# A four-layer graph network on one core: five blocks of the third layer turned by VectorE in the second, and fetched

## The chip, the core and the metric

The kernel runs on one core of one Trainium2 chip. Its time is the device time of one launch in microseconds; "before" is 2893.02 us, the median of three runs between 2892.32 and 2893.67. A profile is taken of one more execution. Engines are named as the profile does: PE is TensorE, PEld its weight loads, DVE is VectorE, ACT is ScalarE, POOL is GpSimd, SP is SyncE, which here only issues DMAs.

## The reference, cut to what matters

Four attention layers over one graph of 4096 nodes with 256 features; each result is added to x and normalised. The third layer is the one that changes:

```python
def _L2_gnn_ref(x, adj, W, a):
    h = x @ W
    e_src = h @ a[:D, 0]
    e_dst = h @ a[D:, 0]
    e = e_src[:, None] + e_dst[None, :]
    e = jnp.where(e > 0, e, NEG_SLOPE * e)
    att_logits = jnp.where(adj > 0, e, MASK_VAL)
    attention = jax.nn.softmax(att_logits, axis=1)
    h_prime = attention @ h
    return jax.nn.elu(h_prime)
...
x = _layernorm(x + _L1_gnn_ref(x, adj, ...), axis=-1)     # second layer
x = _layernorm(x + _L2_gnn_ref(x, adj, ...), axis=-1)     # third layer
```

## The kernel before, in words

x lies in SBUF the whole time, as tile X: 128 partitions (P) by 32 tiles of 128 rows. Rows are also counted in 8 blocks (NB) of 512, four tiles (QB) each. Each layer runs over units (b, j): b is one of 8 blocks of outputs (a "pass"), j a tile of the nodes that are summed over; layers one, three and four have 32 units in a pass, layer two has 64. In each unit ScalarE computes exponentials or activations for 512 columns, VectorE multiplies them by the mask, and TensorE adds the products to sums in PSUM (the function sums).

The second layer (multi_head_attention) keeps LAG = 3 units between scores and sums. In its main loop the order on PE, DVE and ACT is the one in which the code issues the instructions. What is left of pass b-1 (row sums, division, normalisation) is strewn over units of pass b by finish: join_sums at units 7 and 9 (L706, one VectorE addition of 128x1024), row sums at 12, halves at 15 and 18, statistics, and four scale_row at 35, 37, 39 and 41, after which block b-1 of X has its final value of the layer. Block 7 is finished in the third layer, by tail. GpSimd adds the even products of a pass up (L683), and a DMA that accumulates (L689, den<-prob, issued by POOL) adds the odd ones; the two join_sums of the last pass are POOL's too.

The third layer (additive_one) needs x turned, features on partitions, for its projection. In pass 0, turn(n) has TensorE transpose a block: 8 transposes of 128x128 into two PSUM banks (L118), copied out by VectorE and ScalarE (L120). project(n) multiplies it by the weights (L196) and fills V, src and dst, from which unit (b, j) takes its j. fill_row(n) writes a block of src along the free dimension on all partitions: for n > 1 by a DMA to DRAM (L441) and another one that spreads it (L442), both issued by POOL. Blocks 0 and 1 are turned and projected ahead of the units; block n from 2 on is turned at unit j = 4(n-2) of pass 0, projected two units later, and used from unit j = 4n. xp, the pool of turned blocks, has 3 buffers. Only PE has its order by hand in this layer; on the other engines, and on all DMA queues, a scheduler that lies between this code and the chip chooses it. weights(b, j) computes a unit's products (L456 ACT, L458 DVE); the masks come from SP, one DMA for two units (L454: 128 partitions by 2 rows of 512 int32, 512 KB), into 4 buffers.

A second way of turning a block is there before the change, for six blocks of the second and all of the fourth layer: turned_apart. VectorE transposes 32x32 squares (L131, two STREAM_TRANSPOSE a block), one DMA writes the squares to DRAM (L133, far<-squares), and four DMAs, one per quarter of the partitions, read them back turned (L135, xT<-far). The nodes then stand in another order: in tile a of the block, partition 32k + n holds row 128k + 32a + n of the block, and masks and rows have to follow that order. The lines that name it:

```python
far = far.tile([QB, B, QB, KC * P], FP, name="far")
eng.dma_start(far.rearrange("a f q m -> (a f) (q m)"), squares.rearrange("p q c m -> p (q c m)"))
for q in range(QB):
    eng.dma_start(to[q * B:(q + 1) * B], far[:, :, q, :].rearrange("a f m -> f a m"))
```

Of the kernel before, what the change touches and what calls it, by code (L numbers as in the profile page):

```python
# [9 lines left out]
FP = mybir.dt.float32  # L10
# [8 lines left out]
P = 128  # L19
D = 256  # L20
KC = D // P
QB = 4
QW = QB * P
# [5 lines left out]
def kernel(  # L29
# [27 lines left out]
    nc = tc.nc  # L57
    N = x.shape[0]
    NT = N // P
    NB = N // QW  # L60

    def pool(stack, name, bufs, **kw):
        return stack.enter_context(tc.tile_pool(name=name, bufs=bufs, reuse_waits="tile", **kw))
# [15 lines left out]
    X = feat.tile([P, NT, D + 1], FP, name="X")  # L79
# [40 lines left out]
            copies[c](xT[:, c, :], pt)  # L120
        return xT.rearrange("p c (k i) -> p c k i", i=P)

    def turned_apart(squares, far, part, to, eng):

        B = P // QB
        squares = squares.tile([P, QB, KC, P], FP, name="squares")
        far = far.tile([QB, B, QB, KC * P], FP, name="far")
        for c in range(KC):  # L130
            nc.vector.transpose(squares[:, :, c, :].rearrange("p q (k n) -> p k q n", n=B),  # L131
                                part(c).rearrange("p k (q f) -> p k q f", f=B))
        eng.dma_start(far.rearrange("a f q m -> (a f) (q m)"), squares.rearrange("p q c m -> p (q c m)"))  # L133
        for q in range(QB):
            eng.dma_start(to[q * B:(q + 1) * B], far[:, :, q, :].rearrange("a f m -> f a m"))  # L135
        return to.rearrange("p a (c m) -> p c a m", c=KC)

    def block_apart(sb, once, dr, b, eng):
        xT = sb.tile([P, KC * QW], FP, name="xT").rearrange("p (a m) -> p a m", a=QB)
        return turned_apart(once, dr, lambda c: X[:, b * QB:(b + 1) * QB, c * P:(c + 1) * P], xT, eng)  # L140

    def one_row(mv, k, y):
        st = fin.tile([P, 6], FP, name="bn")
# [29 lines left out]
    def scale_row(y, mv, r, k):  # L173
        nc.vector.tensor_scalar(y, y, mv[:, k, 0:1], r[:, k:k + 1], OP.subtract, OP.mult)
# [226 lines left out]
    def additive_one(w_sb, slope, tail, op, follow):  # L401

        MJ = 2
        mvs, taken = {}, {}
        with ExitStack() as lay:
            keep = pool(lay, "gb_keep", 1)
            V = keep.tile([P, NT, D + 1], FP, name="V")
            src = keep.tile([P, NT, 1], FP, name="src")
# [3 lines left out]
            sb = pool(lay, "gb_sb", 2)  # L412
            xp = pool(lay, "gb_turn", 3)
            sq = pool(lay, "gb_squares", 1)
            far = pool(lay, "gb_far", 2, space=bass.MemoryType.DRAM)
# [3 lines left out]
            dr = pool(lay, "gb_dram", 2, space=bass.MemoryType.DRAM)  # L419

            ps = pool(lay, "gb_ps", 4, space=PSUM)
            pa = pool(lay, "gb_pa", 1, space=PSUM)
            edges = adjT.rearrange("(t p) i -> p t i", p=P)
            mask, acc, prob = {}, {}, {}

# [3 lines left out]
            def turn(b):  # L429
                return transposed_block(xp, bank, b)  # L430

            def project(b, xT, ks=range(QB)):
                groups = [(k, 1, bank().rearrange("p (n f) -> p n f", n=1)) for k in ks]
                additive_values(xT, b, groups, w_sb, V, src, dst, 1, slope)

            def fill_row(b):
                part = row[:, b * QW:(b + 1) * QW]
                if b > 1:

                    far = dr.tile([QB, P], FP, name="far")  # L440
                    nc.gpsimd.dma_start(far.rearrange("k p -> p k"), src[:, b * QB:(b + 1) * QB, 0])  # L441
                    nc.gpsimd.dma_start(part, far.rearrange("k p -> (k p)").unsqueeze(0).to_broadcast([P, QW]))  # L442
                    return
                pr = bank()
                for k in range(QB):
                    nc.tensor.transpose(pr[:, k * P:(k + 1) * P], src[:, b * QB + k, :].to_broadcast([P, P]), ident)
                nc.scalar.copy(part, pr)

            def weights(b, j):
                cols = slice(b * QW, (b + 1) * QW)  # L450
                m = b, j // MJ
                if j % MJ == 0:
                    mask[m] = mp.tile([P, MJ, QW], I32, name="mask")
                    nc.sync.dma_start(mask[m], edges[:, j:j + MJ, cols])  # L454
                e = sb.tile([P, QW], FP, name="e")
                nc.scalar.activation(e, row[:, cols], AF.Relu, bias=-1.0, scale=dst[:, j, :])  # L456
                prob[b, j] = zp.tile([P, QW], FP, name="prob")
                nc.vector.scalar_tensor_tensor(prob[b, j], e, 1.0, mask[m][:, j % MJ, :], OP.add, OP.mult)  # L458
# [27 lines left out]
            units = [(b, j) for b in range(NB) for j in range(NT)]  # L486
            with tc.manual_schedule(engines={mybir.EngineType.PE}):
                xTs = {0: turn(0), 1: turn(1)}
                project(0, xTs[0])
                project(1, xTs[1], [0, 1])  # L490
                fill_row(0)
                project(1, xTs[1], [2, 3])
                for i in range(len(units) + 1):
                    if i < len(units):
                        b, j = units[i]
                        weights(b, j)

                        if b == 0 and j // QB + 2 < NB:
                            n = j // QB + 2
                            if j % QB == 0:  # L500
                                xTs[n] = turn(n)
                            elif j % QB == 2:
                                project(n, xTs[n])
                                fill_row(n)
                    if i:
                        b, j = units[i - 1]
                        sums(b, j)
                        if (b, j) == (0, 1):
                            fill_row(1)
                        if b == 0 and j in (0, 3, 5):  # L510
                            tail(bank, (0, 3, 5).index(j))
                            if j == 5:
                                follow.start()
                        if b and j % 4 == 0 and j // 4 < QB:
                            outputs(b - 1, j // 4)
                        n, rest = divmod(i - (NB - 1) * NT + 5, 4)
                        if rest == 0 and 0 <= n < NB - 2:
                            follow.prepare(even_bank, n, 0)
                        if b == NB - 1:
                            if j in (6, 10, 14):  # L520
                                follow.load_mask(0, (j - 6) // 4, prob[b, j][:, :1])


                            for step, first in enumerate((2, 5), 1):
                                if j >= first and (j - first) % 4 == 0 and (j - first) // 4 < NB - 2:
                                    follow.prepare(even_bank, (j - first) // 4, step)
                        if j == NT - 1:
                            take_all(b)
# [7 lines left out]
    def multi_head_attention(w_sb, b_sb, tail, rows_of_den, narrow_edges):  # L536
# [8 lines left out]
        MJ = 4  # L545
# [3 lines left out]
        with ExitStack() as lay:  # L549
# [7 lines left out]
            with ExitStack() as pro:  # L557
                wp = pool(pro, "mh_w", 1)
                sb = pool(pro, "mh_in", 4)
                sq = pool(pro, "mh_sq", 1)  # L560
                dr = pool(pro, "mh_far", 2, space=bass.MemoryType.DRAM)
# [79 lines left out]

            zp = pool(lay, "mh_z", 8)
            mp = pool(lay, "mh_mask", 3)
            ps = pool(lay, "mh_pz", 3, space=PSUM)
            pa = pool(lay, "mh_pa", 1, space=PSUM)
            mask, acc, prob, score = {}, {}, {}, {}
# [112 lines left out]
            def finish(b, j):  # L759

                rows = [X[:, b * QB + k, :D] for k in range(QB)]
                if j in (7, 9):
                    join_sums(b, j // 2 - 2)
                elif j == 12:
                    row_sums(halves(), b)
                elif j == 15:
                    bank = halves()
                    pd = turned_row_sums(bank, b)
                    po = turned_half(bank, b, 0)
                    reciprocals(pd, b)  # L770
                    half(po, b, 0)
                elif j == 18:
                    half(turned_half(halves(), b, 2), b, 2)
                elif j in (21, 23, 25, 27):
                    k = (j - 21) // 2
                    if k == 0:
                        mvs[b] = fin.tile([P, QB, 2], FP, name="mv")
                    one_row(mvs[b], k, rows[k])
                elif j == 29:
                    roots[b] = begin_root(mvs[b])  # L780
                elif j == 31:

                    end_root(*roots[b], nc.gpsimd)
                elif j in (35, 37, 39, 41):
                    k = (j - 35) // 2
                    scale_row(rows[k], mvs[b], roots[b][1], k)

# [38 lines left out]
    class Cosine:  # L828

        MJ = 4  # L830
# [151 lines left out]
        return part[:, t:t + QB, :]  # L982

    w2_sb = const.tile([P, KC, D + 2], FP, name="w2_sb")
    wm_sb, bm_sb = {}, {}
    with ExitStack() as weights1, ExitStack() as den1, ExitStack() as weights3:
        wp = weights1.enter_context(tc.tile_pool(name="w1", bufs=1, side="right"))
# [66 lines left out]
```

## Time and profile before

| | |
|---|---|
| median of three runs | 2893.02 us (2892.32 to 2893.67) |
| the profiled execution | 2893.66 us, span 2891.9 us from its first to its last instruction |
| layer one / start of layer two / its main loop (us of the span) | 0 to 712 / 712 to 806 / 806 to 1710 |
| layer three, pass 0 / passes 1 to 7 | 1710 to 1797 / 1797 to 2210 |
| TensorE busy in pass 0 of layer three (1710 to 1800) | 90.00 of 90.00 us |
| VectorE and POOL busy in the main loop of layer two (904 us) | 690 and 806 us |
| TensorE transposes of x (L118) in the whole kernel | 144, of 272 ns each, pipelined |
| VectorE transposes of squares (L131) | 44, 702 ns each |
| mask loads of layer three (L454) | 128, SP issues one in 0.37 us |
| row fills on POOL: L441, then L442 | 6 of each; 9.7 us and 6.2 us from issue to landing |

How to read the lines below: a page line of the first part gives busy time, its share of the span and the number of instructions. In the chain in order of time a line is start, length, engine, tile, line. A timeline line is start, duration, engine, line, operation, out<-in, and in brackets how long the engine had idled and what ended that. A line of waits is: engine, its line, "<-" what it waited for, then us in total, times, longest. In a table of stages the columns are the stretch, its length, busy time (and instructions) of PE, PEld, DVE, ACT and POOL, granted clock, busy share of the DMA engines and GB/s.

### The profile page before, as it was taken

Reading aid. Unit: us, or ns where it says so; the run is one execution under the profiler, and the core shown is the slowest. Engines: PE = TensorE matmul, PEld = TensorE weight load, DVE = VectorE, ACT = ScalarE, POOL = GpSimd, SP = SyncE. Lnnn points to the kernel's source line nnn. Section 1 sums busy time; section 2 is a strip of 40 time slices with the busy share of each in tenths; the row PEclk is TensorE's granted clock in tenths of the full one; section 3 lists DMA queues with packets and bytes.
Section 4 is the critical chain, followed back from the end, with each engine's and each line's share of the span. In section 5 each row is a group of like instructions: output and inputs, shape, how many; then the busy total and the mean of one; then the engine's idle time right before and its main releaser. Section 6 shows DMA issues by size and latency. Waiting matters only on the chain.

```text
span 2891.9 us, 50575 instructions
## 1 busy us (share of the span) xinstructions
PE 2879.8 (100%) x20093; PEld 1546.5 (53%) x20093; DVE 1960.4 (68%) x2553; ACT 1649.3 (57%) x2577; POOL 946.7 (33%) x705
## 2 busy tenths in 40 slices
PE   9999999999999999999999999999999999999998
PEld 4333333333543333333333358888888777777776
DVE  8899999998777777777777765655667323333333
ACT  7899999997356666666666653444444222222222
POOL 0010010100068988989899870000002000000000
PEclk9999999999999999999999999999999999999999
DMA  7566667675269889889899885565566444344341
GB/s 206 103 139 137 142 133 146 138 133 92 88 138 192 183 187 196 181 188 190 182 193 187 181 178 133 165 185 158 159 185 177 75 58 58 58 58 58 58 59 29
DMA packets 237071, 398.04 MB, mean 138 GB/s; under 512 B 20913, under 2 KB 121249, under 8 KB 235938
## 3 DMA queue, kind: packets, MB, share of 16 engines
q0 software_dynamic: 104320, 184.06, 40.2%
q1 hardware_dynamic: 132240, 210.49, 24.2%
q8 instruction: 157, 2.57, 0.3%
q14 instruction: 80, 0.66, 0.1%
q10 hardware_dynamic: 274, 0.26, 0.0%
HBM read 328.60 MB, written 32.58 MB: 125 GB/s over the span
## 4 chain that ended last, share of the span: by engine, by line
PE 99%; DVE 0%; ACT 0%; DMA 0%; issue 0%; SPq 0%; DVEq 0%; ACTq 0%
PE acc L293 23%; PE p L664 15%; PE acc L922 15%; PE acc L697 15%; PE acc L464 8%; PE g L464 8%; PE p L910 4%; PE g L910 3%; PE g L579 2%; PE g L196 1%; PE pv L598 1%; PE acc L869 1%; PE acc L196 1%; PE g L118 1%; PE g L305 0%; PE p L734 0%
## 5 line engine op out<-in xcount | busy, mean ns | idle before, releaser
L676 DVE TENSOR_TENSOR prob<-p,mask 128x1024 f32<-128x1024 f32 x512 | 624.1, 1223 | 209.3 <-ACT p L666 204.3
L666 ACT ACTIVATE p<-p,shift 128x1024 f32<-128x1024 f32 x512 | 556.2, 1088 | 325.2 <-PE p L664 324.4
L293 PE MATMUL acc<-prob,V 128*32 128x512 f32 x6144 | 664.0, 592 | 1.2 <-DVE prob L283 1.2
L683 POOL TENSOR_TENSOR den<-den,prob 128x1024 f32<-128x1024 f32 x248 | 627.7, 2531 | 73.2 <-DVE prob L676 66.9
L280 ACT ACTIVATE prob<-row,dst 128x512 f32<-128x512 f32 x1020 | 633.2, 713 | 0.1
L283 DVE SCALAR_TENSOR_TENSOR prob<-prob,mask 128x2048 f32<-128x2048 f32 x256 | 582.7, 2288 | 24.1 <-ACT prob L280 21.6
L664 PE MATMUL p<-qT,kT 64*64 64x512 f32 x4096 | 532.3, 590 | 0.8 <-DVE prob L676 0.8
L697 PE MATMUL acc<-prob,V 64*64 64x512 f32 x4096 | 531.5, 589 | 0.0
L922 PE MATMUL acc<-X,prob 128*128 128x257 f32 x2048 | 485.4, 380 | 0.0
L922 PEld LDWEIGHTS acc<-X,prob 128*128 128x128 f32 x2048 | 388.7, 190 | 162.6 <-issue 113.6
L915 DVE TENSOR_TENSOR prob<-prob,mask 128x512 f32<-128x512 f32 x256 | 176.3, 691 | 410.4 <-ACT prob L914 409.3
L293 PEld LDWEIGHTS acc<-prob,V 128*32 128x32 f32 x6144 | 197.3, 110 | 453.0 <-issue 431.7
L91 POOL COPY tick<-prob 128x1 f32<-128x1 f32 x35 | 40.0, 1143 | 996.6 <-DVE prob L283 644.8
L456 ACT ACTIVATE e<-row,dst 128x512 f32<-128x512 f32 x256 | 183.9, 721 | 244.2 <-DVE prob L458 215.4
L697 PEld LDWEIGHTS acc<-prob,V 64*64 64x64 f32 x4096 | 155.9, 133 | 285.4 <-issue 278.1
L664 PEld LDWEIGHTS p<-qT,kT 64*64 64x64 f32 x4096 | 154.4, 133 | 277.3 <-issue 261.5
L458 DVE SCALAR_TENSOR_TENSOR prob<-e,mask 128x512 f32<-128x512 f32 x256 | 177.3, 693 | 169.2 <-PE acc L464 91.6
L854 POOL DMA_DIRECT2D mask<-in_adjT x64 | 47.5, 742 | 585.1 <-DVE prob L915 519.0
L689 POOL DMA_DIRECT2D den<-prob x240 | 231.6, 965 | 15.0 <-DVE prob L676 5.9
L914 ACT ACTIVATE prob<-p 128x512 f32<-128x512 f32 x144 | 85.7, 596 | 260.1 <-PE p L910 246.0
L464 PE MATMUL acc<-V,prob 128*128 128x257 f32 x1024 | 225.1, 380 | 0.0
L464 PE MATMUL g<-V,prob 128*128 128x257 f32 x1024 | 223.7, 380 | 0.0
(159 smaller groups left out, 1934.4 us busy)
## 6 DMA issues: line engine op xcount, KB each, us to landing
mask<-in_adjT SPq DMA_DIRECT2D x256, 512.0 KB
den<-prob POOLq DMA_DIRECT2D x240, 512.0 KB, 5.1
mask<-edges SPq DMA_DIRECT2D x512, 64.0 KB
mask<-in_adjT POOLq DMA_DIRECT2D x64, 512.0 KB, 5.7
edges<-in_adj POOLq DMA_DIRECT2D x32, 512.0 KB, 10.0
far<-squares SPq DMA_DIRECT2D x16, 512.0 KB
den<-prob SPq DMA_DIRECT2D x16, 512.0 KB
row<-far SPq DMA_DIRECT2D x7, 1024.0 KB
```

Source lines behind the costliest of these rows:

```text
L280: nc.scalar.activation(z[:, h, :], r, AF.Relu, bias=-1.0, scale=dst[:, j, h:h + 1])
L283: nc.vector.scalar_tensor_tensor(z, z, 1.0, mask[m][:, j % MJ, :].unsqueeze(1).to_broadcast([P, H, QW]), OP.add, OP.mult)
L293: nc.tensor.matmul(acc[b][h * G:(h + 1) * G, n, :], part, prob[b, j][:, h, :], start=(j == 0), stop=(j == NT - 1))
L464: nc.tensor.matmul(acc[b][k][:, :D + 1], prob[b, j][:, k * P:(k + 1) * P], V[:, j, :], start=(j == 0), stop=(j == NT - 1))
L664: nc.tensor.matmul(p[c * d:(c + 1) * d, r, :], kT[half, c, at:at + d], qT[half, c, cols], start=True, stop=True)
L666: nc.scalar.activation(p, p, AF.Exp, bias=shift)
L676: nc.vector.tensor_tensor(z, p, mask[m][:, j % MJ, :].unsqueeze(1).to_broadcast([P, KC, QW]), OP.mult)
L683: nc.gpsimd.tensor_tensor(to, to, flat, OP.add)
L689: nc.gpsimd.dma_start(to, flat, accum_op=OP.add)
L697: nc.tensor.matmul(acc[b][c][r * d:(r + 1) * d, :], V[half, j, r * d:(r + 1) * d], prob[b, j][half, r, :], start=(j == 0), stop=(j == NH - 1))
L910: nc.tensor.matmul(p.rearrange("p (k i) -> p k i", k=QB), T[j // QB][:, 0, j % QB], T[b][:, 1], start=True, stop=True)
L922: nc.tensor.matmul(acc[b][k], prob[b, j][:, k * P:(k + 1) * P], X[:, j, :], start=(j == 0), stop=(j == NT - 1))
```

## The change

turned_apart is cut in two: squares_of (VectorE's transposes and the DMA to DRAM) and squares_placed (the four DMAs back). The second layer's finish gets a step at unit 44: for block b from 2 on it runs squares_of on the finished X, so that blocks 2 to 6 (finish doesn't reach block 7, and 0 and 1 are left out) lie as squares in DRAM when the third layer begins. There fetch(n), four DMAs on POOL's queue, replaces turn(n) for these blocks: fetch(2) ahead of everything, fetch(n + 1) where turn(n) stood. Blocks 0, 1 and 7 are still turned by TensorE. Since nodes in the fetched blocks stand in the other order, fill_row for blocks 2 to 6 writes src to DRAM with four DMAs for quarters of the partitions, then spreads it as before, and a mask of two units in these blocks (j from 8 to 27) is loaded by four DMAs of 32 partitions, 128 KB each.

```diff
--- before.py
+++ after.py
@@ -120,7 +120,7 @@
             copies[c](xT[:, c, :], pt)
         return xT.rearrange("p c (k i) -> p c k i", i=P)
-    def turned_apart(squares, far, part, to, eng):
+    def squares_of(squares, far, part, eng):
@@ -131,13 +131,25 @@
             nc.vector.transpose(squares[:, :, c, :].rearrange("p q (k n) -> p k q n", n=B),
                                 part(c).rearrange("p k (q f) -> p k q f", f=B))
         eng.dma_start(far.rearrange("a f q m -> (a f) (q m)"), squares.rearrange("p q c m -> p (q c m)"))
+        return far
+
+    def squares_placed(far, to, eng):
+        B = P // QB
         for q in range(QB):
             eng.dma_start(to[q * B:(q + 1) * B], far[:, :, q, :].rearrange("a f m -> f a m"))
         return to.rearrange("p a (c m) -> p c a m", c=KC)
+    def turned_apart(squares, far, part, to, eng):
+        return squares_placed(squares_of(squares, far, part, eng), to, eng)
+
+    def chunk(b):
+        return lambda c: X[:, b * QB:(b + 1) * QB, c * P:(c + 1) * P]
+
+    def new_xT(sb):
+        return sb.tile([P, KC * QW], FP, name="xT").rearrange("p (a m) -> p a m", a=QB)
+
     def block_apart(sb, once, dr, b, eng):
-        xT = sb.tile([P, KC * QW], FP, name="xT").rearrange("p (a m) -> p a m", a=QB)
-        return turned_apart(once, dr, lambda c: X[:, b * QB:(b + 1) * QB, c * P:(c + 1) * P], xT, eng)
+        return turned_apart(once, dr, chunk(b), new_xT(sb), eng)
     def one_row(mv, k, y):
         st = fin.tile([P, 6], FP, name="bn")
@@ -420,6 +432,7 @@
             ps = pool(lay, "gb_ps", 4, space=PSUM)
             pa = pool(lay, "gb_pa", 1, space=PSUM)
+            apart = adjT.rearrange("(b k a n) i -> k n b a i", k=QB, a=QB, n=P // QB)
             edges = adjT.rearrange("(t p) i -> p t i", p=P)
             mask, acc, prob = {}, {}, {}
@@ -428,6 +441,9 @@
             def turn(b):
                 return transposed_block(xp, bank, b)
+
+            def fetch(b):
+                return squares_placed(turned[b], new_xT(xp), nc.gpsimd)
             def project(b, xT, ks=range(QB)):
                 groups = [(k, 1, bank().rearrange("p (n f) -> p n f", n=1)) for k in ks]
@@ -437,9 +453,14 @@
                 part = row[:, b * QW:(b + 1) * QW]
                 if b > 1:
-                    far = dr.tile([QB, P], FP, name="far")
-                    nc.gpsimd.dma_start(far.rearrange("k p -> p k"), src[:, b * QB:(b + 1) * QB, 0])
-                    nc.gpsimd.dma_start(part, far.rearrange("k p -> (k p)").unsqueeze(0).to_broadcast([P, QW]))
+                    far = dr.tile([QB, QB, P // QB], FP, name="far")
+                    if b < NB - 1:
+                        for k in range(QB):
+                            at = slice(k * P // QB, (k + 1) * P // QB)
+                            nc.gpsimd.dma_start(far[k].rearrange("a n -> n a"), src[at, b * QB:(b + 1) * QB, 0])
+                    else:
+                        nc.gpsimd.dma_start(far.rearrange("k a n -> (a n) k"), src[:, b * QB:(b + 1) * QB, 0])
+                    nc.gpsimd.dma_start(part, far.rearrange("k a n -> (k a n)").unsqueeze(0).to_broadcast([P, QW]))
                     return
                 pr = bank()
                 for k in range(QB):
@@ -451,7 +472,13 @@
                 m = b, j // MJ
                 if j % MJ == 0:
                     mask[m] = mp.tile([P, MJ, QW], I32, name="mask")
-                    nc.sync.dma_start(mask[m], edges[:, j:j + MJ, cols])
+                    if j // QB in turned:
+
+                        for k in range(QB):
+                            nc.sync.dma_start(mask[m][k * P // QB:(k + 1) * P // QB],
+                                              apart[k, :, j // QB, j % QB:j % QB + MJ, cols])
+                    else:
+                        nc.sync.dma_start(mask[m], edges[:, j:j + MJ, cols])
                 e = sb.tile([P, QW], FP, name="e")
                 nc.scalar.activation(e, row[:, cols], AF.Relu, bias=-1.0, scale=dst[:, j, :])
                 prob[b, j] = zp.tile([P, QW], FP, name="prob")
@@ -486,6 +513,7 @@
             units = [(b, j) for b in range(NB) for j in range(NT)]
             with tc.manual_schedule(engines={mybir.EngineType.PE}):
                 xTs = {0: turn(0), 1: turn(1)}
+                xTs[2] = fetch(2)
                 project(0, xTs[0])
                 project(1, xTs[1], [0, 1])
                 fill_row(0)
@@ -497,7 +525,9 @@
                         if b == 0 and j // QB + 2 < NB:
                             n = j // QB + 2
-                            if j % QB == 0:
+                            if j % QB == 0 and n + 1 in turned:
+                                xTs[n + 1] = fetch(n + 1)
+                            elif j % QB == 0 and n + 1 == NB:
                                 xTs[n] = turn(n)
                             elif j % QB == 2:
                                 project(n, xTs[n])
@@ -641,6 +671,7 @@
             zp = pool(lay, "mh_z", 8)
             mp = pool(lay, "mh_mask", 3)
+            sq = pool(lay, "mh_squares", 1)
             ps = pool(lay, "mh_pz", 3, space=PSUM)
             pa = pool(lay, "mh_pa", 1, space=PSUM)
             mask, acc, prob, score = {}, {}, {}, {}
@@ -784,6 +815,8 @@
                 elif j in (35, 37, 39, 41):
                     k = (j - 35) // 2
                     scale_row(rows[k], mvs[b], roots[b][1], k)
+                elif j == 44 and b > 1:
+                    turned[b] = squares_of(sq, turned_far, chunk(b), nc.sync)
@@ -982,6 +1015,9 @@
         return part[:, t:t + QB, :]
     w2_sb = const.tile([P, KC, D + 2], FP, name="w2_sb")
+
+    turned = {}
+    turned_far = ctx.enter_context(tc.tile_pool(name="turned", bufs=NB - 3, space=bass.MemoryType.DRAM))
     wm_sb, bm_sb = {}, {}
     with ExitStack() as weights1, ExitStack() as den1, ExitStack() as weights3:
         wp = weights1.enter_context(tc.tile_pool(name="w1", bufs=1, side="right"))
```

## The prediction

> **What bounds the kernel now.** I read the page's busy shares and its chain that ended last, then that chain in order of time where layer two meets layer three, then, for the same stretch, the timelines of POOL and DVE, the tables of waits, and the busy time by stage.
>
> ```profile
> PE 2879.8 (100%) x20093; PEld 1546.5 (53%) x20093; DVE 1960.4 (68%) x2553; ACT 1649.3 (57%) x2577; POOL 946.7 (33%) x705
> ...
> PE 99%; DVE 0%; ACT 0%; DMA 0%; issue 0%; SPq 0%; DVEq 0%; ACTq 0%
> ```
>
> TensorE is the end, everywhere: a microsecond counts if TensorE stops doing it, or starts waiting.
>
> ```profile
> 1717.72 0.44 PE g L446 x4
> 1718.16 1.75 PE g L196 x8
> 1719.90 0.87 PE g L118 x8
> 1720.78 1.74 PE acc L464 x8
> 1722.51 3.49 PE g L196 x16
> ...
> 1754.62 0.87 PE g L118 x8
> 1755.49 3.47 PE acc L464 x16
> ```
>
> Read here: eight transposes of one block (L118) hold TensorE for 0.87 us, a unit of sums (L464) 1.74, a projection of a block (L196) 3.49. (This chain counts to ends; the timeline gives starts, some 0.16 us earlier.)
>
> ```profile
> 1711.73 2.36 POOL L706 TENSOR_TENSOR den<-den 128x1024 f32<-128x1024 f32 x1 [1.42 <-DMA den<-prob]
> 1714.03 0.87 POOL L689 DMA_DIRECT2D den<-prob  x1
> 1722.57 2.41 POOL L706 TENSOR_TENSOR den<-den 128x1024 f32<-128x1024 f32 x1 [7.67 <-DMA den<-prob]
> 1727.66 0.84 POOL L441 DMA_DIRECT2D far<-src  x1 [2.69 <-ACT V L202]
> 1737.49 0.55 POOL L442 DMA_DIRECT2D row<-far  x1 [8.99 <-DMA far<-src]
> 1739.04 0.77 POOL L441 DMA_DIRECT2D far<-src  x1 [0.99 <-ACT V L202]
> 1749.92 0.54 POOL L442 DMA_DIRECT2D row<-far  x1 [10.12 <-DMA far<-src]
> ```
>
> POOL is the queue that the fetches join. Its busy time is small, but it blocks for 8 to 10 us at a time on landings. Note too that the first L706 stands before the last L689, though the program writes it later: POOL's order isn't that of the text.
>
> ```profile
> 1389.05 1.23 DVE L676 TENSOR_TENSOR prob<-p,mask 128x1024 f32<-128x1024 f32 x1 [0.56 <-ACT p L666]
> 1390.19 1.22 DVE L706 TENSOR_TENSOR den<-den 128x1024 f32<-128x1024 f32 x1
> 1391.32 2.37 DVE L676 TENSOR_TENSOR prob<-p,mask 128x1024 f32<-128x1024 f32 x2
> ...
> SPq L454 <- DVE prob L458: 273.3, 84, 7.6
> ...
> 1800.00:2133.00 333.00, 333.00 (x1538) 291.42 (x1537) 194.83 (x426) 147.97 (x229) 0.00 (x0) 1.00 0.58 168
> 2133.00:2210.00 77.00, 77.00 (x357) 67.54 (x356) 56.32 (x129) 39.47 (x145) 20.08 (x37) 1.00 0.82 214
> ```
>
> The first three lines are layer two: VectorE idles about half a microsecond in each unit. The fourth says what SP waits for when it loads masks of layer three: the multiplication that frees a buffer. The last two are layer three's passes, TensorE busy throughout, DMA engines 0.58 busy at 168 GB/s, and 0.82 in the last pass.
>
> [...] by its packet records, the 1 KB packets that L135 writes into 32 partitions between 730 and 800 us took 46 ns in the median but 91 at the ninth decile, about double. [...] In this trace the last accumulation (L689, issued 1714.03) moves its packets from 1717.9 to 1722, as the four mask loads of SP's queue run out[...].
>
> **The change part by part.**
>
> *Transposes leave TensorE.* Five blocks (2 to 6) lose 8 transposes: 5 x 0.87 = 4.35 us, the most that the change can give, 0.15%. Not all of it comes. The first set (1719.90) fills a time in which the first sums couldn't start: the first L458 ends at 1720.26 by VectorE's timeline, and hangs on fill_row's transposes, ScalarE's copy of the row and its first activation, none of which change. TensorE is free at 1719.74 by its timeline and starts those sums at 1720.62 now; it can start at about 1720.35. That set yields 0.3, the other four 0.87 each, as TensorE has no gap around them: 0.3 + 3.5 = 3.8 us. The ten PSUM copies that go from VectorE and ScalarE (0.68 and 0.62 us each) give nothing, neither ends a wait of TensorE there.
>
> *Transposes enter layer two.* Five times two STREAM_TRANSPOSE of 0.70 us, 1.30 us back to back, at unit 44 of passes 3 to 7. VectorE's multiplications queue behind them, and TensorE waits for those. The nearest row is L706: 1.22 us slipped between two multiplications, caught up from the idle half microseconds, while TensorE's units kept their 1.717 us from start to start. Bounds: 0 and 0.4 us each (a delay of 1.3 minus the idle 0.42 to 0.56 left in two units); below nothing is excluded, since nothing is removed there. I take 0, for the low end holds in the nearest case. The 512 KB written by SP is 128 packets of 4 KB at 159 to 185 ns over 16 engines, 1.3 us of DMA per pass where the queues are 0.90 busy; the accumulations that it delays free buffers of which there are eight (13.7 us of units), and land in 5.1. Nothing. SP's masks behind this issue are loaded two groups ahead, 8 units or 13.7 us.
>
> *Fetches on POOL.* Each is four DMAs of 128 KB at 0.55 us of issue (row L135 on POOL) and 4.5 us to landing. A fetch needs only the block's data, long in DRAM, and one of three buffers: fetch 2 a region that layer two leaves at 1710.6 (the first masks, SP, wait for the same moment), fetches 3 and 4 the buffers of blocks 0 and 1, free once those are projected (1716 and 1720). Needed: projection 2 at 1722.05 (1722.35 less 0.3), 3 at 1734.6, 4 at 1745.4, 5 at 1755.9, 6 at 1766.3. If fetches go out when their buffers are free, 3 to 6 have 10 us or more to spare. Fetch 2 hasn't. I place it behind the L689 of 1714.03, since that depends on VectorE's last product, a little before TensorE's last use of the region. Then it is issued from 1714.9 to 1717.1, [...] 512 packets of 1 KB at 46 to 60 ns over 16 engines take 1.7 more: 1724.1. TensorE's order is written by hand, so everything behind projection 2 waits: 2.05 us. Bounds: 0, if fetch 2 goes ahead of L689; 9, if it stands behind the second L706 (issue to 1727.2, landing near 1731). I take 2. The row sums at 1732.5 need that second L706, which ends at 1725.0, so that up to 6 us of delay on POOL is hidden there.
>
> *Row fills.* Two DMAs become five for blocks 2 to 6: four of 0.56 to 0.77 us instead of one. The rows are first read in pass 2, at about 1856 us; nothing waits, except fetches queued behind.
>
> *Masks.* 80 of 128 loads become four of 128 KB: 240 more issues at 0.37 us. SP then spends 1.5 us per two units of 3.47 us. It waits for buffers now, so that each load leaves six units before its use (6 x 1.735 = 10.4, about 11 with the rest of a unit)[...]. At the doubled packet time (2 x 84 ns for 2 KB, 16 packets per engine) a group takes 2.7 us of the 3.47: not the bound. Nothing.
>
> *Waits.* Projections wait for four landings instead of two copies: some 51 ns events on TensorE's queue (the L118 waits took 51). Between 0 and 0.8 us in all; I take 0.3.
>
> Sum against the profiled execution (2893.66 us; its span 2891.9): -3.8 + 2.0 + 0.3 = -1.5. Its own time lies 0.6 above the median of 2893.02, so I apply the difference to the median: 2891.5.
>
> **Rivals.**
> 1. *No wait for fetch 2*: it goes out ahead of L689 and lands near 1720. -3.8 + 0.3: 2889.5. For it: POOL is idle from 1710.3 to 1711.7. Against: the product that L689 needs comes before the region is free.
> 2. *POOL's queue takes the place of the transposes* (slower). If POOL keeps the program's order, fetch n+2 stands behind both DMAs of fill_row n, and so behind the landing of 8.99 to 10.12 us. The four issues (2.8 us), the landing (9.7), the broadcast (0.55) and the fetch (2.2) make 15 us a block; TensorE takes 10.4. Stepping on: fill_row 2 starts at 1727.7, fetch 4 is issued by 1742.7 and lands at 1747.2 (needed 1745.4, wait 1.8); fetch 5 lands at 1762.7 (needed 1757.7, wait 5); fetch 6 at 1778.1 (needed 1773.1, wait 5). Waits of 11.8 against 3.8 gained: 2901. It decides once a block's POOL work exceeds the 10.4 us, which it does if the order is so. Against it: the L706 ahead of L689; and SP's first far<-squares for layer four went out at 2043.8, some 80 us ahead of its place in the program (unit 219, near 2125), so instructions are placed when they are ready.
> 3. *Fetch 2 behind the second L706*: a wait of 9: 2893 - 3.8 + 9 = 2898.2.
> 4. *The quarters bound layer three*: DMA in the last pass is 0.82 busy. If a quarter's packets took three times 84 ns, a group needs 4.0 us against 3.47, 0.56 x 80 = 45 less the cover: about 2925. Against it: 91 ns, not 250, in the nearest transfers.
>
> **How the numbers follow.** About 0.2%, 5.8 us, is what a measurement can tell from no change. Chances: the forecast 0.45, rival 1 0.22, rival 2 0.20, rival 3 0.06, rival 4 0.05, the rest 0.02. Forecast, rival 1 and almost all of rival 3 are within 0.2%: 0.72. Rivals 2, 4 and the upper part of 3 are slower: 0.25. Faster by 5.8 us would need more than all the transposes: 0.03. The forecast's own range is 2889.5 to 2893.5 (the wait for fetch 2, 0 to 3, and 0.8 of waits); to leave out no more than 2 in 10 it must take in rival 3 and half of rival 2: 2889 to 2901.
>
> **What would show it.** No L118 between 1719 and 1777 but one set; layer two's span unchanged to 1 us (else the transposes on VectorE cost); one TensorE wait of about 2 us before projection 2, released by a DMA xT<-far, and none before 3 to 6 (waits of 2 to 5 us before 4, 5 and 6 are rival 2, with POOL's L135 behind L442); SP's mask loads still waiting for VectorE, not VectorE for masks. I am wrong if TensorE waits for masks, or if layer two grows.

## The result, and the profile after

The changed kernel takes 2919.95 us (median of four runs, 2919.56 to 2920.86) against 2892.67 for the kernel before: a ratio of 1.0093, 95% interval 1.008 to 1.0105. It is 27 us slower, where 2891.5, "no change", was forecast, in a range of 2889 to 2901.

The page of the changed kernel: the engines' busy time, and the chain that ended last.

```profile
PE 2884.3 (99%) x20053; PEld 1546.5 (53%) x20053; DVE 1960.8 (67%) x2558; ACT 1646.9 (56%) x2572; POOL 965.7 (33%) x740
...
PE 96%; DVE 2%; ACT 1%; DMA 1%; issue 0%; POOL 0%; DVEq 0%; ACTq 0%; POOLq 0%
```

TensorE has 40 instructions fewer, but the chain is now 96% TensorE instead of 99: VectorE, ScalarE and DMAs stand in it, so TensorE waits. A share says little of where. The starts of TensorE's sums at the same units in the two traces do. (Pass 1 starts at 1803.97 here, not at 1797 as the table of the profile before has it.)

| stretch, by TensorE's starts | before, us | after, us | difference |
|---|---|---|---|
| up to unit (1, 0) of layer three | 1803.97 | 1809.51 | +5.54 |
| units (1, 0) to (7, 0), six passes | 333.08 | 333.08 | 0.00 |
| units (7, 0) to (7, 31), the last pass | 74.49 | 95.97 | +21.48 |
| from there to the end | 680.32 | 679.26 | -1.06 |
| span | 2891.86 | 2917.81 | +25.96 |

Two places, then, and between them six passes with quarter masks that cost TensorE nothing at all.

**The first place.** The timeline of TensorE after, then that of POOL. Columns: start, length, engine, line, operation and tiles, and in brackets the idle time ahead and what ended it. L208 is the projection, L491 the sums, L737 the addition of row sums, L720 the accumulating DMA, L139 the fetch (L196, L464, L706, L689 and L135 before).

```profile
1719.79 2.00 PE L491 MATMUL acc<-V,prob 128*128 128x257 f32 x8 [0.41 <-DVE prob L485]
1729.64 5.40 PE L208 MATMUL g<-w_sb,xT 128*128 128x258 f32 x16 [7.85 <-DMA xT<-far]
1734.88 1.90 PE L491 MATMUL acc<-V,prob 128*128 128x257 f32 x8
```

```profile
1712.60 2.35 POOL L737 TENSOR_TENSOR den<-den 128x1024 f32<-128x1024 f32 x1 [1.91 <-DMA den<-prob]
1714.89 0.88 POOL L720 DMA_DIRECT2D den<-prob  x1
1722.10 2.68 POOL L737 TENSOR_TENSOR den<-den 128x1024 f32<-128x1024 f32 x1 [6.33 <-DMA den<-prob]
1724.73 4.98 POOL L139 DMA_DIRECT2D xT<-far  x9
```

The fetch stands behind the second addition, which itself waited for the accumulation to land, and is issued at 1724.73, when TensorE had been waiting for it for 3 us. The wait is 7.85 us. And then the projection takes 5.24 us from start to start, where the same sixteen matmuls took 3.49. The table of stages shows why. Its columns are the stretch, its length, busy time of PE, PEld, DVE, ACT and POOL, TensorE's granted clock, the busy share of the DMA engines, GB/s:

```profile
1720.00:1726.00 6.00, 1.79 (x8) 1.22 (x7) 2.33 (x5) 1.92 (x3) 3.90 (x4) 1.00 0.57 156
1726.30:1733.00 6.70, 3.36 (x8) 2.74 (x9) 0.42 (x1) 0.90 (x4) 3.41 (x7) 0.50 0.63 171
1733.10:1740.00 6.90, 6.90 (x35) 6.03 (x35) 2.66 (x5) 2.33 (x12) 3.25 (x6) 1.00 0.08 19
2180.30:2187.00 6.70, 5.89 (x14) 4.70 (x15) 2.74 (x5) 2.78 (x4) 0.56 (x1) 0.50 1.07 250
2197.30:2204.00 6.70, 4.51 (x11) 3.59 (x12) 4.01 (x7) 2.06 (x3) 1.33 (x3) 0.50 1.11 263
```

TensorE's clock is granted at 0.50 from 1726.2 us, during the wait, to 1733.0 us, and at 1.00 after that. So the first half of the projection ran at half pace: the clock fell 4.4 us after TensorE had stopped (1721.8) and came back 3.4 us after it had started again (1729.64); the longest of the projections' matmuls between 1715 and 1735 us took 771 ns, the median 381. So a wait of 7.85 us cost 9.6. Counted by starts, from the first sums to the second, it is 15.09 us instead of 5.22, 9.87 more. Less the 0.83 us that the first sums came earlier, and 3.50 for the four sets of transposes that are gone behind them, this makes the +5.54 of the table.

**The second place.** VectorE in the last pass: first a piece of the kernel before, then the piece for the same kind of block after. L875/L908 copy the projected rows of layer four's preparation out of PSUM, L880/L913 scale them, L131 turns them; L458/L485 is the multiplication by the mask, which layer three's sums wait for.

```profile
2166.14 0.69 DVE L875 COPY rows<-acc 128x512 f32<-128x512 f32 x1 [2.11 <-ACT sq L874]
2167.93 0.69 DVE L875 COPY rows<-acc 128x512 f32<-128x512 f32 x1 [1.09 <-ACT sq L874]
2168.54 0.16 DVE L877 TENSOR_SCALAR v<-norm 128x8 f32<-128x8 f32 x1
2168.61 0.69 DVE L458 SCALAR_TENSOR_TENSOR prob<-e,mask 128x512 f32<-128x512 f32 x1
...
2170.02 1.22 DVE L880 TENSOR_TENSOR rows<-rows,r 128x1024 f32<-128x1024 f32 x1
2171.16 0.68 DVE L458 SCALAR_TENSOR_TENSOR prob<-e,mask 128x512 f32<-128x512 f32 x1
2171.85 1.31 DVE L131 STREAM_TRANSPOSE squares<-rows 128x512 f32<-128x512 f32 x2
```

```profile
2174.01 0.69 DVE L908 COPY rows<-acc 128x512 f32<-128x512 f32 x1 [3.18 <-ACT sq L907]
2175.80 0.69 DVE L908 COPY rows<-acc 128x512 f32<-128x512 f32 x1 [1.09 <-ACT sq L907]
...
2177.91 1.22 DVE L913 TENSOR_TENSOR rows<-rows,r 128x1024 f32<-128x1024 f32 x1
2179.17 1.30 DVE L131 STREAM_TRANSPOSE squares<-rows 128x512 f32<-128x512 f32 x2
2180.40 1.25 DVE L485 SCALAR_TENSOR_TENSOR prob<-e,mask 128x512 f32<-128x512 f32 x2
```

Before, a multiplication stands between copy and scaling and another between scaling and transposes. After, all of the block's chain comes first, and the multiplications follow. The chain hangs on TensorE's own projection for layer four, by way of ScalarE, so TensorE waits for work that its own result set off:

```profile
2170.91 3.62 PE L902 MATMUL acc<-w_sb,xT 128*128 128x256 f32 x16
2174.36 1.90 PE L491 MATMUL g<-V,prob 128*128 128x257 f32 x8
2181.11 8.37 PE L491 MATMUL g<-V,prob 128*128 128x257 f32 x24 [4.85 <-DVE prob L485]
2189.31 3.62 PE L902 MATMUL acc<-w_sb,xT 128*128 128x256 f32 x16
2192.76 1.90 PE L491 MATMUL g<-V,prob 128*128 128x257 f32 x8
2199.49 7.72 PE L491 MATMUL g<-V,prob 128*128 128x257 f32 x24 [4.82 <-DVE prob L485]
```

One unit of sums after the projection (L902), then nothing for 4.8 us, and the clock is low again after it (0.50 in the last two lines of the table above; 24 matmuls take 8.4 and 7.7 us instead of 5.4). Nothing in the change names VectorE in this pass; the mask loads are all that it alters there. The order is the scheduler's. The theories to test: A, the mask loads by quarters change that order; B, the late fetch moves the rest; C, quarters arrive late.

### The profile page after: what moved, and what is told of

Its sections match the earlier page's. It is cut to its first block, busy times and chain, and to the rows that moved or that the text cites. A ratio compares the mean times of both kernels' runs of the same rounds, so it can differ in the third digit from the quotient of the medians.

```text
span 2917.8 us, 50968 instructions
## 1 busy us (share of the span) xinstructions
PE 2884.3 (99%) x20053; PEld 1546.5 (53%) x20053; DVE 1960.8 (67%) x2558; ACT 1646.9 (56%) x2572; POOL 965.7 (33%) x740
## 4 chain that ended last, share of the span: by engine, by line
PE 96%; DVE 2%; ACT 1%; DMA 1%; issue 0%; POOL 0%; DVEq 0%; ACTq 0%; POOLq 0%
PE acc L305 23%; PE acc L955 15%; PE p L695 15%; PE acc L728 15%; PE acc L491 8%; PE g L491 7%; PE p L943 4%; PE g L943 3%; PE g L609 2%; PE g L208 1%; PE pv L628 1%; PE acc L208 1%; PE acc L902 0%; DMA den<-prob 0%; PE g L317 0%
## 5 line engine op out<-in xcount | busy, mean ns | idle before, releaser
L714 POOL TENSOR_TENSOR den<-den,prob 128x1024 f32<-128x1024 f32 x248 | 635.8, 2564 | 69.4 <-DVE prob L707 62.6
L295 DVE SCALAR_TENSOR_TENSOR prob<-prob,mask 128x2048 f32<-128x2048 f32 x256 | 582.6, 2287 | 24.2 <-ACT prob L292 21.5
L485 DVE SCALAR_TENSOR_TENSOR prob<-e,mask 128x512 f32<-128x512 f32 x256 | 175.3, 687 | 176.2 <-PE acc L491 90.0
L491 PE MATMUL g<-V,prob 128*128 128x257 f32 x1024 | 230.4, 386 | 13.1 <-DVE prob L485 13.1
L720 POOL DMA_DIRECT2D den<-prob x240 | 236.4, 985 | 18.9 <-DVE prob L707 8.5
L491 PE MATMUL acc<-V,prob 128*128 128x257 f32 x1024 | 224.5, 380 | 0.4 <-DVE prob L485 0.4
```

The costliest lines, as they stand in the source:

```text
L295: nc.vector.scalar_tensor_tensor(z, z, 1.0, mask[m][:, j % MJ, :].unsqueeze(1).to_broadcast([P, H, QW]), OP.add, OP.mult)
L491: nc.tensor.matmul(acc[b][k][:, :D + 1], prob[b, j][:, k * P:(k + 1) * P], V[:, j, :], start=(j == 0), stop=(j == NT - 1))
L714: nc.gpsimd.tensor_tensor(to, to, flat, OP.add)
L720: nc.gpsimd.dma_start(to, flat, accum_op=OP.add)
```

## The experiments

Each time is a median, each ratio one of the runs beside runs of the kernel before on the same chip. "Last pass" is from TensorE's first matmul of unit (7, 0) to that of unit (7, 31), from the trace.

**Quarters alone**, in the kernel before:

```diff
-                    nc.sync.dma_start(mask[m], edges[:, j:j + MJ, cols])
+                    if 1 < j // QB < NB - 1:
+                        for k in range(QB):
+                            at = slice(k * P // QB, (k + 1) * P // QB)
+                            nc.sync.dma_start(mask[m][at], edges[at, j:j + MJ, cols])
+                    else:
+                        nc.sync.dma_start(mask[m], edges[:, j:j + MJ, cols])
```

> The kernel before, with one edit: masks of units 8 to 27 of the third layer are loaded by four DMAs of 32 partitions, rows in the old order. Theory A (with four DMAs for one, the scheduler lays VectorE's instructions of the last pass in another order, and the multiplications stand behind the preparation of layer four): the last pass of layer three takes 90 to 96 us from its first to its last unit instead of 74.5, the other passes stay at 55.5, total about 2913. Theory B (the late fetch moves the rest): 2893, last pass 74.5. Theory C (transfers into a quarter of the partitions arrive late): as A in time, but VectorE waits for mask DMAs.

Measured: 2915.09 us, ratio 1.0077 (1.006 to 1.0094); last pass 95.64 us, the six passes before it 333.08, as in the kernel before. From the table of waits of the last pass:

```profile
DVE rows L880 <- ACT sq L879: 21.9, 6, 6.3
PE g L469 <- DVE prob L463: 13.5, 5, 4.8
```

TensorE waits five times for VectorE's product, 13.5 us in all, two of the waits 4.82. In that pass no wait of VectorE for a mask shows; it waits 21.9 us for ScalarE's squares. B falls: there is no fetch here. So does C as the cause.

**Whole masks** in the changed kernel:

```diff
-                    if j // QB in turned:
-
-                        for k in range(QB):
-                            nc.sync.dma_start(mask[m][k * P // QB:(k + 1) * P // QB],
-                                              apart[k, :, j // QB, j % QB:j % QB + MJ, cols])
-                    else:
-                        nc.sync.dma_start(mask[m], edges[:, j:j + MJ, cols])
+                    nc.sync.dma_start(mask[m], edges[:, j:j + MJ, cols])
```

> The changed kernel, with each mask loaded by one DMA again; in the five fetched blocks mask rows then stand in the old order, which leaves the re-ordering of the mask out. Theories A and C: the last pass is back at 74.5 us, total about 2899. Theory B: stays at 2920.

Measured: 2901.80 us, ratio 1.003 (1.0018 to 1.0042); last pass 74.49 us, as before. What is left is the first place, where the wait was even 9.79 us in this trace; unit (1, 0) starts 9.47 us later than before. A later projection waited 0.51 us.

**The first fetch on SP**:

```diff
-            def fetch(b):
-                return squares_placed(turned[b], new_xT(xp), nc.gpsimd)
+            def fetch(b, eng=nc.gpsimd):
+                return squares_placed(turned[b], new_xT(xp), eng)
...
-                xTs[2] = fetch(2)
+                xTs[2] = fetch(2, nc.sync)
```

> The changed kernel, with the first fetch (block 2) issued by SP instead of POOL. If the wait of 7.85 us before the second projection comes from the place in POOL's queue behind the second addition of row sums: the wait falls below 1 us, and with it the slower matmuls after it, total about 2911. If it comes from the DMA engines being full at that time: a wait of 4 us or more stays, about 2916.

Measured: 2910.53 us, ratio 1.0061 (1.0046 to 1.0076). SP's timeline and TensorE's in this run:

```profile
1710.42 2.26 SPq L139 DMA_DIRECT2D xT<-far  x4
```

```profile
1721.47 3.66 PE L208 MATMUL g<-w_sb,xT 128*128 128x258 f32 x16
```

The fetch goes out 14 us earlier than on POOL, the projection starts without a wait, and at full pace. It was the place in the queue, not full DMA engines; in the changed kernel too the four DMAs of this fetch landed within 3.1 us of their issue. The last pass stays at 96.10. A new wait of 1.87 us shows before block 6, whose fetch is on POOL.

**The same, and layer four's preparation off SP**; the masks stay in quarters:

```diff
-                self.xT[b] = block_apart(*self.turning, b, nc.sync)
+                self.xT[b] = block_apart(*self.turning, b, nc.gpsimd)
```

> As the run before, and the squares and fetches that prepare layer four in the last pass go to POOL's queue instead of SP's; the masks stay in quarters. In this kernel the order laid out for VectorE in the last pass has multiplications between the preparations again. Theory A: last pass near 75 us, total 2889 to 2893. Theory C: the quarters are still late, total about 2910.

Measured: 2891.58 us, ratio 0.9994 (0.9986 to 1.0003); last pass 75.41. The same 128 KB transfers into the same partitions, and no wait of TensorE in the pass. POOL's queue still costs before block 6, 1.51 us at TensorE; the timelines of TensorE and POOL:

```profile
1767.73 3.73 PE L208 MATMUL g<-w_sb,xT 128*128 128x258 f32 x16 [1.51 <-issue]
```

```profile
1758.51 0.56 POOL L463 DMA_DIRECT2D row<-far  x1 [8.80 <-DMA far<-src]
1759.06 0.56 POOL L139 DMA_DIRECT2D xT<-far  x1
1759.60 0.55 POOL L460 DMA_DIRECT2D far<-src  x1
```

A last part of the fetch stood behind a row fill that blocked the queue for 8.80 us, and then took 8.5 us to land, at 1767.53, just ahead of the projection. The profile names no releaser for this wait; that it was the fetch is read from this landing.

**The order alone**, in the kernel before, with whole masks and no fetch; for blocks 2 and 3 of layer four the next multiplication is put behind the block's transposes (turned_last[0] holds the last transpose that was written, and issue_after puts an instruction behind it):

```diff
-                nc.vector.scalar_tensor_tensor(prob[b, j], e, 1.0, mask[m][:, j % MJ, :], OP.add, OP.mult)
+                with tc.issue_after(hold[0]) if hold[0] is not None else nullcontext():
+                    nc.vector.scalar_tensor_tensor(prob[b, j], e, 1.0, mask[m][:, j % MJ, :], OP.add, OP.mult)
+                hold[0] = None
...
-                                    follow.prepare(even_bank, (j - first) // 4, step)
+                                    n = (j - first) // 4
+                                    if n not in (2, 3) or step == 1:
+                                        follow.prepare(even_bank, n, step)
+                                    if n in (2, 3) and step == 1:
+                                        follow.prepare(even_bank, n, 2)
+                                        hold[0] = getattr(turned_last[0], "ins", turned_last[0])
```

> The kernel before, with masks whole and no fetch; only the order on VectorE is forced in the last pass: for two blocks of layer four (2 and 3), the multiplication that follows is put behind the scaling and the transposes of that block, as it stands in the changed kernel. If this order is the cause, two waits of TensorE of about 4.8 us and the slower matmuls after each, as in the run of quarters alone, where two such blocks made units 8 to 16 of the pass 14.7 us longer: about 2908. If the order only goes along with late masks: 2893 to 2896.

Measured: 2905.99 us, ratio 1.0044 (1.0028 to 1.006); last pass 87.94, 13.45 longer. TensorE in this run:

```profile
2172.07 7.13 PE L468 MATMUL g<-V,prob 128*128 128x257 f32 x24 [4.82 <-DVE prob L461]
2179.03 3.62 PE L878 MATMUL acc<-w_sb,xT 128*128 128x256 f32 x16
2182.49 1.90 PE L468 MATMUL g<-V,prob 128*128 128x257 f32 x8
2189.20 7.09 PE L468 MATMUL g<-V,prob 128*128 128x257 f32 x24 [4.82 <-DVE prob L461]
```

The two waits of 4.82 us are there to the hundredth, and each block costs 6.7 us with the slow matmuls. This is the mechanism without a narrow transfer in it, but not the whole amount: 13.45 of the 21.15 us that the quarters alone add to the pass. The other three waits of that run, 3.8 us, stand at blocks whose order is not forced here, and the clock is at 0.50 for 3.4 us after each long wait here, for 6.8 us there.

**How many DMAs it takes.** Halves instead of quarters in the kernel before, and quarters in all passes but the last:

```diff
-                        for k in range(QB):
-                            at = slice(k * P // QB, (k + 1) * P // QB)
+                        for k in range(2):
+                            at = slice(k * P // 2, (k + 1) * P // 2)
```

> The kernel before, with masks of units 8 to 27 loaded by two DMAs of 64 partitions. The order laid out for VectorE in the last pass is that of before here. If the order is what costs: 2893. If more and narrower mask DMAs cost by themselves, some part, a third or more, of the 22 us of the quarters: 2900.

Measured: 2893.70 us, ratio 1.0001 (0.9993 to 1.001); last pass 74.50.

```diff
-                    if 1 < j // QB < NB - 1:
+                    if 1 < j // QB < NB - 1 and b < NB - 1:
```

> The kernel before, with masks of units 8 to 27 in quarters in passes 0 to 6, and whole in the last pass. If quarters cost only through the order in the last pass, where they stand beside the preparation of layer four: 2893 to 2895. If they cost in every pass: 2905 or more.

Measured: 2894.32 us, ratio 1.0003 (0.9995 to 1.0012); last pass 77.01, with waits of 1.45 and 0.50 us. Two DMAs a mask leave VectorE's order as it was; four, beside the preparation in the last pass, don't. Even quarters that end before the last pass move some of it: SP writes the first squares for layer four at 2126.7 us, as in the run of quarters alone (2126.8), where it is 2043.8 in the kernel before. VectorE's transposes of x for the first two of these blocks, at 2041.9 and 2097.4 us in the kernel before, then stand at 2134.5 and 2145.5, and the last pass takes 2.5 us more.

**The transposes in layer two alone**: the changed kernel without fetches, with masks and row fills as before.

```diff
-                    if b < NB - 1:
+                    if False:
                         for k in range(QB):
...
-                    if j // QB in turned:
+                    if False:
...
-                xTs[2] = fetch(2)
...
-                            if j % QB == 0 and n + 1 in turned:
-                                xTs[n + 1] = fetch(n + 1)
-                            elif j % QB == 0 and n + 1 == NB:
+                            if j % QB == 0:
                                 xTs[n] = turn(n)
```

> The changed kernel with only the layer-two part left: VectorE turns the five blocks and SP writes them to DRAM, but the third layer turns all blocks on TensorE, with masks and row fills as before. If the transposes on VectorE are hidden in layer two, as the prediction had it: same as before, 2892 to 2894. If each pushes TensorE by up to 0.4 us: up to 2895.

Measured: 2893.01 us, ratio 0.9998 (0.999 to 1.0006). In the main loop of layer two VectorE is busy 4.5 us longer (694.8 against 690.3), and from TensorE's first scores of layer two to its first transposes of layer three it is 900.70 us in both kernels. Hidden, as forecast.

**Towards a version that gains.** All fetches on SP, with the preparation on POOL:

```diff
-            def fetch(b, eng=nc.gpsimd):
+            def fetch(b, eng=nc.sync):
```

> As the run with the first fetch on SP and the preparation of layer four on POOL, but all five fetches are issued by SP. If the wait of 1.5 us before the sixth block's projection comes from POOL's queue, where the fetch stands behind a row fill's landing: no wait of TensorE for a fetch, about 2.5 to 4 us below before, 2889 to 2890.5. If SP's queue holds them up instead: waits of 1 us or more at blocks 3 to 6, 2892 or more.

Measured: 2892.15 us, ratio 0.9996 (0.9988 to 1.0005). No wait for a fetch, but one of 0.85 us for a product in pass 0; the expected gain was missed. The profile's chain runs from that product to a quarter of a mask that SP issued at 1739.36, right behind the four DMAs of a fetch (1735.13 to 1738.37), and that landed at 1744.08. So SP's queue did hold something up, a mask and not a fetch.

Fetches and preparation on SP, quarters in turn from SP and ScalarE:

```diff
-                            nc.sync.dma_start(mask[m][k * P // QB:(k + 1) * P // QB],
+                            (nc.scalar if k % 2 else nc.sync).dma_start(mask[m][k * P // QB:(k + 1) * P // QB],
```

> The changed kernel with all fetches on SP, and the quarters of a mask issued in turn by SP and ScalarE; the preparation of layer four stays on SP. The order laid out for VectorE in the last pass has multiplications between the preparations. If the order is the cause: last pass below 78 us, total 2889 to 2894. If the count of mask DMAs is: 2905 or more. ScalarE also waits for mask buffers here, so a few us may be lost in all passes.

Measured: 2892.99 us, ratio 1.0002 (0.9993 to 1.001); last pass 75.26. Again quarters without the loss, now with the preparation left on SP, whose first squares go out at 2048.9 us. TensorE waited 0.79 us in pass 0, 0.45 in pass 1 and 0.39 in the last, and passes 1 and 2 were 0.7 us and 0.2 us longer. The twelve times spread more than elsewhere, from 2890.77 to 2902.04.

Preparation on POOL; blocks 2, 5 and 6 fetched by SP, 3 and 4 by POOL:

```diff
-            def fetch(b, eng=nc.gpsimd):
+            def fetch(b, eng=None):
+                eng = eng or (nc.gpsimd if b < 5 else nc.sync)
```

> As the runs with the preparation of layer four on POOL; blocks 2, 5 and 6 are fetched by SP, 3 and 4 by POOL. If each of the two earlier versions lost 1.5 us and 0.9 us to the queue that its late fetches stood in, this one has no wait of TensorE for a fetch or a mask and comes to 2889 to 2890. If SP's fetches hold up the masks again: 2891 to 2892.5.

Measured: 2890.82 us (median of 21 runs), ratio 0.9992 (0.9985 to 0.9998). In layer three one wait of TensorE is left, 0.41 us before the first sums. At unit (2, 0) it is 3.74 us ahead of before, near all of the removed transposes; the last pass gives 1.0 us back (75.48 against 74.49). It is 0.08% faster than the kernel before, only just clear of no change, and 1.0% faster than the changed kernel.

## Why the prediction was wrong

- *Transposes leave TensorE: 0.3 + 3.5 us.* Right. The first sums start 0.83 us earlier; 0.53 of this was there before layer two began (its first scores start at 809.29 against 809.82) and isn't the change's, which leaves 0.30. From unit (0, 1) to (1, 0) the lag falls from 9.04 to 5.54: 3.50.
- *Transposes enter layer two: 0.* Right: layer two takes the same 900.70 us before, in the changed kernel and in the run of them alone.
- *Fetch 2: a wait of 2.05.* Wrong place in the queue. It was put behind L689 because its buffer should be free before the second L706 could start; it stands behind that L706. This was rival 3, priced at 9 and given 0.06; the wait was 7.85. The 2.05 us also took the fetch to move only after the accumulation of L689 had landed, at 1722.4: the author's assumption, which no run shows. The price of rival 3 lacked the clock: 1.75 us more for the matmuls after it, 9.6 in all. The wait on SP's queue is zero.
- *Fetches 3 to 6: no wait.* In the changed kernel true, as everything was late. With fetch 2 on time, block 6 waited 1.51 and 1.87 us behind a row fill: a small piece of rival 2, which in full (a wait at each of blocks 4 to 6, 11.8 us) did not come. The landing was priced at 4.5 us; in the changed kernel it took 2.9 to 3.3 for the DMAs issued up to 1729.1 and 6.2 to 9.1 for those from 1737.7 on. (Projection 3 was needed at 1733.7, not 1734.6, as block 3's transposes go too; nothing hangs on it.)
- *Waits for landings: 0.3.* Too small to see.
- *Masks: "Nothing".* This step failed most. For TensorE it holds in passes 1 to 6, where quarters cost 0.00 us of 333. The 11 us by which a load leaves before its use were only just enough: VectorE waited for a mask six times in the window from 1800 to 2133 us, 1.0 us at most; in the kernel before it waited for none, and the prediction's signs had none. The doubled packet time, the author's estimate from 46 and 91 ns, did not come in most packets either: between 1805 and 2040 us the 2 KB packets took 84 ns in the median both before and in the changed kernel, and 166 against 126 at the ninth decile. But the step asked only what the extra DMAs do to SP and to the transfers. It did not ask what they do to the order that the scheduler lays out where SP has other work to place: the preparation of layer four in the last pass. That cost 21.5 of the 26 us; without the quarters the changed kernel takes 2901.80, not 2919.95. The prediction used the fact that the scheduler moves instructions (SP's first far<-squares 80 us ahead of its place), and argued from it only in its favour. In the changed kernel the first of them in that stretch went out at 2131.8 instead of 2043.8.
- Rival 4 looked at the right instruction and pass with the wrong mechanism: transfers three times as long, where the waits were for a multiplication placed late.

Shown: the quarters bring the loss (put in alone, taken out alone), the order on VectorE by itself brings 13.45 us of it (forced alone, for two blocks), and narrow transfers without that order don't bring it (four runs, last pass 75.26 to 75.48). The traces tie the rest to the order too: written out for the last pass, VectorE's order of multiplications, copies, scalings and transposes is one and the same in the changed kernel, in quarters alone and with the first fetch on SP; with whole masks and with halves it is that of the kernel before. In the former, the two blocks behind which the long waits stand have no multiplication between the first copy and the last transpose. That the remaining 7.7 us come from the order of the other blocks was not tested by itself. Why the scheduler turns the order between two and four DMAs a mask is not shown, only that it goes away when SP has less to issue in that pass.

## What to carry to other kernels

Where a scheduler orders the queues, an edit can cost in two places: where its instructions stand, and wherever the same queue serves something else; after adding DMAs, compare the order of every engine with that of before, most of all on an engine that a hand-written order waits for. A fetch that TensorE needs early should not stand in a queue that blocks on landings (POOL's for 6.33 us here): the same four DMAs cost 9.6 us behind POOL's addition and nothing on SP. And price a long wait of TensorE with the slow matmuls that follow it: here waits of 4.82 us and more had them, waits of up to 1.87 us had none.

## What the runs showed of the hardware

- After a wait of 7.85 us TensorE's granted clock stood at 0.50 for the first 3.4 us of work, and sixteen matmuls took 1.75 us longer. Equal waits did not cost the same: after 4.82 us it stood at 0.50 for 3.4 us of work in the run of the order alone, for 5.9 and 4.6 us after 4.85 and 4.82 in the changed kernel, where 24 matmuls took 3.0 and 2.35 us longer (8.37 and 7.72 instead of 5.37). After waits of 1.51 and 1.87 us it stayed at 1.00.
- Loads of 128 KB into 32 partitions, four in place of one of 512 KB, kept up with the masks (512 KB in two units of 1.735 us, which makes 151 GB/s): TensorE lost nothing in six passes, though VectorE waited for a mask six times, 1.0 us at most.
- The same DMA of a fetch, 128 KB on POOL's queue, landed after 2.9 to 3.3 us when issued up to 1729.1, and after 6.2 to 9.1 us when issued between the row fills from 1737.7 on. What makes the difference is not shown.
